# Inner products of text tokens in four 32-column strips instead of one 128-column product

## The chip, the cores and the metric

The kernel runs on one core of one Trainium2 chip. The metric is the device time of one execution in microseconds (us); a kernel's time is the median over its runs. The engines are PE (matrix products; PEld is its weight load), DVE (vector), ACT (scalar), POOL (GpSimd) and SP, which here only issues DMAs.

## The reference

The reference is a cross-attention layer with text tokens and four image-prompt tokens per batch: 8 batches, 112 query rows, 320 channels, 20 heads of 16, 371 text tokens and 4 prompt tokens of 512 numbers each, all float32.

```python
q = heads(hidden_states @ W_q)
k_t = heads(text_ehs @ W_k)
v_t = heads(text_ehs @ W_v)
probs_t = jax.nn.softmax(jnp.einsum('bhsd,bhtd->bhst', q, k_t) * attn_scale, axis=-1)
text_out = jnp.einsum('bhst,bhtd->bhsd', probs_t, v_t)
...
attn_scores = jnp.einsum('bhsd,bhnd->bhsn', q, k_ip) * attn_scale
qsem = _l2norm(jnp.einsum('bhst,bte->bhse', probs_t, text_ehs))
sem = jnp.einsum('bhse,bne->bhsn', qsem, _l2norm(ip_ehs))
probs_ip = jax.nn.softmax(attn_scores + SEM_SCALE * sem, axis=-1)
probs_ip = probs_ip * spatial_mask[None, None, :, None]
out = text_out + jnp.einsum('bhsn,bhnd->bhsd', probs_ip, v_ip)
out = out @ W_out + b_out + residual
```

What matters here is the norm of `qsem`. Its square is p G p, where p is one row of probabilities and G the 371 x 371 matrix of inner products of the batch's text tokens. The kernel computes G once per batch, and uses only its upper triangle, with the entries above the diagonal doubled.

## The kernel before, in words

For each batch the context is transposed into `ctxT`: 128 partitions, 4 chunks `e` of the embedding, 384 token columns, of which 371 are text, 4 are the normalised prompts (L380) and 9 are zero. The 384 tokens are taken in three chunks `c` of 128 rows (NT = 3), and each of these in four blocks `q` of 32 rows (QN = 4, RG = 32), which makes twelve blocks `j` (BLK).

`gram(b)` (L453 to 469, batches 1 to 7) computes the inner products. For each chunk `c` it takes one PSUM bank and issues four products (L461), one per embedding chunk: the weights are the 128 token columns of the chunk, and all columns from the chunk's first to the prompts stream by (375, 247 and 119 of them). They accumulate in the bank. `doubled` (L445) then copies the bank to the tile `ug` on ACT with a factor 2 (L450), and on POOL multiplies the 128 columns of the diagonal chunk with the mask `half` (L451), which has 0.5 in the four diagonal blocks and 1 elsewhere. `half` is set up in the prologue (L172 to 175). Batch 0 has a function of its own, `first_gram`.

`gram_to_groups` (L471) copies 32 rows of `ug` at a time by DMA into `u`, for each of four partition groups: block position `q` of `u` holds those rows for all three chunks. `values` (L525) computes the value vectors into `vext`; `values_to_dram` (L548) writes them to DRAM, all three chunks in one DMA for odd batches, two and then one for even ones; `values_to_groups` (L554) reads them back into `vr`, and `placed` (L602) puts each group's values behind the rows of `u` on POOL (L606). `region(b, c)` (L373) is the part of `u` that belongs to chunk `c`.

A step is one batch and one group of four heads. `product(b, g, j, heads)` (L684, L690) multiplies, for each head `a`, the transposed probabilities of block `j` with `u`'s rows of that block, from the block's diagonal on (L693): 32 partitions of weights per head, so that four heads lie in four row strips of PE's array. `scores` (L639) works in the same strips. The result, 392 columns for block 0 and 40 for block 11, holds p G, the prompts' products, the sum of p and the weighted values.

The order on PE, ACT, POOL, SP and DVE is written out by hand. `pair(n)` (L1125) runs two groups and the scores and probabilities of later ones (two groups ahead); `behind(n)` (L1192) puts what the next batch needs behind every second group: keys (`k`, L499 and L490), queries (`q`, L334), values (`v`, L533), inner products (`gr`), pieces of the finish of the batch before (`f`, L902 and L914). For odd batches the inner products stand between `k` and `v`; for even ones they stand last, behind `f` or `k`, and the next `pair` follows. Behind batch 1's inner products stands the projection of the prompts (L270), whose weights are 32 columns wide. SP's queue carries, in the order written, the probabilities to the transposes (L665), the copies of `ug` (L475), the values (L549, L558), the contexts (L138, L143) and the results (L883).

Of the kernel before, what the change touches and what calls it, by code (L numbers as in the profile page):

```python
# [8 lines left out]
F32 = mybir.dt.float32  # L9
AF = mybir.ActivationFunctionType  # L10
ALU = mybir.AluOpType
# [9 lines left out]
def kernel(  # L21
# [14 lines left out]
    nc = tc.nc  # L36
    P = 128
    B, S, C = x.shape
    T, E = ehs.shape[1:]
# [5 lines left out]
    NE = E // P  # L45
# [5 lines left out]
    RG = 32  # L51
# [11 lines left out]
    QN = P // RG  # L63
# [3 lines left out]
    UCOL = QN * GW  # L67
    assert (H, D, NC, NT, P) == (20, 16, 3, 3, 128) and RG == 2 * D


    groups = [[i * HC + 2 * a + r for a in range(GROUP)] for i in range(2) for r in range(2)]
    groups.append([2 * HC + a for a in range(GROUP)])

    const = ctx.enter_context(tc.tile_pool(name="const", bufs=1))
# [11 lines left out]
    def bank(name, spare=False):  # L86

        tag = turn.pop(0) if turn else "sc" if spare else "mm"
        return pools[tag].tile([P, 512], F32, tag=tag, name=name)
# [79 lines left out]
    make_identity(nc, ident)  # L169
    nc.gpsimd.memset(wq_sb[REST:, FULL, :], 0.0)  # L170

    half = const.tile([P, P], F32, tag="half", name="half")  # L172
    nc.gpsimd.memset(half, 1.0)
    for q in range(QN):
        nc.gpsimd.memset(half[q * RG : (q + 1) * RG, q * RG : (q + 1) * RG], 0.5)

    hmask = const.tile([P, HC], F32, tag="hmask", name="hmask")
    nc.vector.tensor_reduce(
# [28 lines left out]
    k3 = const.tile([P, NT, GROUP, 2, D], F32, tag="k3", name="k3")  # L207

    def more_constants():
        nc.gpsimd.memset(k3[:, :, :, 1, :], 0.0)  # L210
        nc.gpsimd.memset(wo_sb[REST:, FULL, :], 0.0)
        for at in attn_ring:
            nc.gpsimd.memset(at[:, C:], 0.0)
# [137 lines left out]
    st = {}  # L351
# [21 lines left out]
    def region(b, c):  # L373

        u = st[b]["u"].rearrange("p (q w) -> p q w", w=GW)
        return u[:, :, GCOL[c] : GCOL[c + 1]]
# [46 lines left out]
    def first_gram():  # L423

        ctxT = st[0]["ctxT"]
        banks = []
        for c in range(NT):
            banks.append(ps_qd.tile([P, 512], F32, tag="qd", name=f"ps_g_0_{c}"))
            if c == NT - 1:
                nc.gpsimd.tensor_copy(ctxT[:, :, TT:T], ipnT[:, :, :NIP])  # L430
            c0, c1 = c * P, min(c * P + P, T)
            for r in range(c + 1):
                for e in range(NE):
                    nc.tensor.matmul(
                        banks[r][:, c0 - r * P : c1 - r * P],
                        ctxT[:, e, r * P : (r + 1) * P],
                        ctxT[:, e, c0:c1],
                        start=(e == 0),
                        stop=(e == NE - 1),
                    )  # L440
                if c == NT - 1:
                    doubled(banks[r], r)
                yield

    def doubled(ps, c):  # L445

        t0 = c * P
        k = min(P, TT - t0)
        g = ug[:, GCOL[c] : GCOL[c] + T - t0]
        nc.scalar.mul(g, ps[:, : T - t0], 2.0)  # L450
        nc.gpsimd.tensor_tensor(g[:, :k], g[:, :k], half[:, :k], ALU.mult)  # L451

    def gram(b):  # L453

        ctxT = st[b]["ctxT"]

        for c in range(NT):
            t0 = c * P
            ps = bank(f"ps_g_{b}_{c}")
            for e in range(NE):  # L460
                nc.tensor.matmul(  # L461
                    ps[:, : T - t0],
                    ctxT[:, e, t0 : t0 + P],
                    ctxT[:, e, t0:T],
                    start=(e == 0),
                    stop=(e == NE - 1),
                )
            doubled(ps, c)
            yield

    def gram_to_groups(b, blocks):  # L471
# [74 lines left out]
            yield  # L546

    def values_to_dram(b, eng, c0=0, c1=NT):  # L548
        eng.dma_start(  # L549
            st[b]["vd"][c0 * P : c1 * P].rearrange("(c p) x -> p c x", p=P),  # L550
            st[b]["vext"][:, c0:c1, :C],
        )

    def values_to_groups(b):  # L554
        s = st[b]
# [128 lines left out]
    def product(b, g, j, heads):  # L684
        s = st[b]
        xT = s["xT", g]
        banks = s["qd", g]
        c, q = j // QN, j % QN
        for a in heads:
            nc.tensor.matmul(  # L690
                banks[a][:S, j * RG : UW],
                xT[a * RG : (a + 1) * RG, j, :S],
                region(b, c)[a * RG : (a + 1) * RG, q, q * RG :],  # L693
                start=(j == 0),
                stop=(j == BLK - 1),
            )
# [8 lines left out]
    def multiplied(b, g):  # L705

        turned_round = b == B - 1 and g % 2 and g < NG - 1
        products_in(b, g, ("mm", "mm", "sc", "sc") if turned_round else ("qd",) * GROUP)
        for j in range(BLK):
            product(b, g, j, range(GROUP))  # L710
            yield
        del st[b]["xT", g]
# [316 lines left out]
    prompts = normalised_prompts()  # L1029
    context = transposed_context(0)  # L1030
    products = first_gram()
    next(prompts)
    awake(4)
# [10 lines left out]
    run(("q", 0), lambda: project_queries(pairs[0]), 3)  # L1044
    run(("v", 0), None, 2)
    values_to_dram(0, nc.scalar)
    spread(nc.gpsimd, wq_sb)
    nc.gpsimd.tensor_copy(wv_sb[:, :, C:], wk_sb[:, :, FULL * P : C])
# [22 lines left out]
    drain(transposed_context(1))  # L1071
    prompts_behind(1)
    more_constants()
    prologue.close()

# [16 lines left out]
    def gr(b, pieces=1):  # L1092
        run(("g", b), lambda: gram(b), pieces)
# [31 lines left out]
    def pair(n):  # L1125
# [7 lines left out]
        for j in range(BLK - 2):  # L1133
            product(b, g, j, range(GROUP))
            if j < 2:
                heads = (HIGH, LOW)[j]
                coming_scores(n + LEAD, heads, tags[j])
                coming_probabilities(n + LEAD, heads)
            if j == 1:
                transposed(*two, BLK // 2, BLK)  # L1140
            if j % QN == QN - 1:
                placed(*two, (j // QN,))
        products_in(*two, (tags[1],) * 2 + (tags[0],) * 2)
        for there, here in ((HIGH, LOW), (LOW, HIGH)):
            product(*two, 0, there)
            for j in ends:
                product(b, g, j, here)
# [44 lines left out]
    def behind(n):  # L1192
# [31 lines left out]
        elif b % 2 == 0 and g == 2:  # L1224
# [10 lines left out]
            if b == 0:  # L1235
                run(("pp",), None)
            tr(1)
            values_to_dram(nb, nc.sync)
        elif b % 2 == 0:
            new = nb < B - 1  # L1240
# [20 lines left out]
        elif g == 1:  # L1261
            turn[:] = ["qd"] * 4 + ["mm"]
            gram_to_groups(nb, (2,))
            q(b)
            k(b)
            k(nb)
            tr(0)
            f(b - 1)
            v(nb)
            tr(1)  # L1270
            v(nb)
            f(b - 1, 3)
            values_to_dram(nb, nc.sync, 0, 2)
            if b == B - 3:
                prompt_values_by_head()
        else:
            turn[:] = ["qd"] * 3 + ["sc"]
            v(nb)
            f(b - 1)
            values_to_dram(nb, nc.sync, 2)  # L1280
            tr(0)
            k(nb)
            f(b - 1, 2)
            tr(1)
            values_to_groups(nb)
        assert not turn, (b, g, turn)

    for n in range(0, len(steps) - NG, 2):
# [4 lines left out]
        b, g = steps[n]  # L1293
# [16 lines left out]
    b = B - 1  # L1310
# [12 lines left out]
    for g in range(NG):  # L1323
# [20 lines left out]
        if g < NG - 1:  # L1344

            n = GROUP - 1 if g <= LEAD else 1
# [89 lines left out]
```

## Time and profile before

| what | value |
|---|---|
| median of 3 runs | 431.86 us (431.05 to 434.98) |
| the profiled execution | 431.93 us |
| its span, first to last instruction | 430.2 us |
| PE, DVE, ACT, POOL busy | 420.1, 328.3, 190.0, 111.1 us |
| L690, products with u | 216.8 us of PE |
| L461, inner products of batches 1 to 7 | 36.9 us of PE |
| moved by DMA | 64.21 MB |

The span is a little shorter than the time, since the time includes the start and the end of the program. A row of a group names the line, the engine, what it writes and reads, the shape (for PE: rows*columns of the weights, then what streams by), the count, the busy time, the mean of one in ns, and the idle time of the engine before it with what ended it. In the order of time a row starts with its start and its length in us. A row of waits has the sum, the number of times and the longest. PE's instructions overlap, so the length of one is not what it costs; the distance from one start to the next is.

### The profile page before, as it was taken

To read this page: it belongs to the slowest core of one execution; us is meant where nothing else is said; L and a number is where in the kernel's file an instruction comes from. 1 tells how busy PE (TensorE), PEld (TensorE's weight loads), DVE (VectorE), ACT (ScalarE), POOL (GpSimd) and SP (SyncE) were. 2 spreads that over 40 slices of the span, in tenths; PEclk is the share of its full clock that TensorE was granted. 3 is DMA by queue.
4 is the path that set the end of the run, shared out by engine and by line. 5 is a ranking of instruction groups with operands and counts; after the bars stand their busy time and mean duration, and the time that the engine had idled before them with its cause. 6 is when DMAs were issued, how large, how long until landed. Compare 5 with 4: busy or idle time off the path is not lost. (4 is left out here: it accounts for less than half of the span.)

```text
span 430.2 us, 12955 instructions
## 1 busy us (share of the span) xinstructions
PE 420.1 (98%) x5011; PEld 322.3 (75%) x5011; DVE 328.3 (76%) x687; ACT 190.0 (44%) x647; POOL 111.1 (26%) x267
## 2 busy tenths in 40 slices
PE   8999999999999999999999999999999999999986
PEld 8756686878677796868687897768786887776783
DVE  4045387987989886887989897795888897778884
ACT  2254141524632642515543553333643463346793
POOL 4302110021160352021061243002142226026440
PEclk9999999999999999999999999999999999999999
DMA  7669946568564655667644566485754436663300
GB/s 240 182 173 266 216 121 160 159 150 197 137 166 113 175 126 138 170 152 168 173 124 134 163 143 156 141 194 122 171 163 120 127 99 165 180 152 105 95 5 28
DMA packets 57547, 64.21 MB, mean 149 GB/s; under 512 B 18368, under 2 KB 51512, under 8 KB 57486
## 3 DMA queue, kind: packets, MB, share of 16 engines
q1 hardware_dynamic: 56920, 62.66, 57.4%
q8 instruction: 40, 0.66, 0.7%
q10 hardware_dynamic: 566, 0.72, 0.5%
q14 instruction: 21, 0.17, 0.1%
HBM read 18.67 MB, written 5.32 MB: 56 GB/s over the span
## 5 line engine op out<-in xcount | busy, mean ns | idle before, releaser
L690 PE MATMUL ps_qd<-u,xgT 32*112 32x104 f32 (+11 forms) x3840 | 216.8, 352 | 2.0 <-POOL u L606 1.7
L690 PEld LDWEIGHTS ps_qd<-u,xgT 32*112 32x112 f32 x3840 | 182.0, 172 | 35.8 <-issue 8.0
L679 DVE STREAM_TRANSPOSE xgT<-xg 128x768 f32<-128x768 f32 (+1 forms) x63 | 121.2, 1952 | 12.3 <-DMA xg<-p 12.2
L656 ACT ACTIVATE p<-ps_s,nmx 112x371 f32<-112x371 f32 x160 | 85.6, 585 | 54.8 <-DVE nmx L652 53.2
L750 DVE CUSTOM_DVE_ANT_0 junk<-ps_qd,p 112x371 f32<-112x371 f32 x148 | 80.1, 541 | 30.6 <-ACT pvs L717 11.4
L652 DVE TENSOR_REDUCE nmx<-ps_s 112x1 f32<-112x371 f32 x160 | 77.2, 535 | 26.7 <-PE ps_s L639 24.7
L606 POOL COPY u<-vr 128x64 f32<-128x64 f32 x120 | 26.5, 236 | 192.7 <-PE ps_qd L690 111.5
L533 PE MATMUL ps_v<-wv_sb,ctxT 128*128 128x384 f32 (+1 forms) x192 | 63.5, 477 | 0.3 <-ACT kT L506 0.3
L639 PE MATMUL ps_s<-kT,qm 32*112 32x375 f32 (+1 forms) x320 | 62.1, 486 | 1.0 <-ACT shared L735 0.7
L533 PEld LDWEIGHTS ps_v<-wv_sb,ctxT 128*128 128x128 f32 x192 | 35.4, 190 | 20.7 <-ACT kT L506 1.2
L717 ACT COPY pvs<-ps_qd 112x21 f32<-112x21 f32 x150 | 21.3, 199 | 61.3 <-DVE ss L750 60.0
L499 PE MATMUL ps_k<-ctxT,wk_sb 128*128 128x371 f32 x136 | 45.8, 481 | 0.0
L461 PE MATMUL ps_g<-ctxT 128*128 128x375 f32 (+2 forms) x168 | 36.9, 376 | 0.7 <-POOL ctxT L380 0.7
L461 PEld LDWEIGHTS ps_g<-ctxT 128*128 128x128 f32 x168 | 28.2, 191 | 9.7 <-POOL ctxT L380 1.2
L499 PEld LDWEIGHTS ps_k<-ctxT,wk_sb 128*128 128x128 f32 x136 | 24.6, 190 | 13.4 <-issue 0.5
L639 PEld LDWEIGHTS ps_s<-kT,qm 32*112 32x112 f32 x320 | 28.1, 171 | 6.9 <-ACT shared L735 1.3
L540 ACT COPY vext<-ps_v 128x384 f32<-128x384 f32 (+1 forms) x24 | 11.2, 465 | 37.1 <-PE ps_v L533 37.0
L658 ACT COPY ipl<-ps_s 112x4 f32<-112x4 f32 x140 | 24.1, 172 | 0.0
L450 ACT ACTIVATE ug<-ps_g 128x375 f32<-128x375 f32 (+2 forms) x24 | 9.0, 376 | 30.4 <-PE ps_g L461 16.5
L506 ACT COPY kT<-ps_k 128x371 f32<-128x371 f32 x17 | 8.0, 469 | 31.0 <-PE ps_k L499 31.0
L343 DVE TENSOR_SCALAR qm<-ps_q,emask 128x224 f32<-128x224 f32 (+1 forms) x25 | 9.0, 397 | 14.9 <-PE ps_q L334 14.9
L451 POOL TENSOR_TENSOR ug<-ug,half 128x128 f32<-128x128 f32 (+1 forms) x24 | 10.7, 447 | 34.5 <-ACT ug L450 34.3
(161 smaller groups left out, 324.9 us busy)
## 6 DMA issues: line engine op xcount, KB each, us to landing
xg<-p SPq DMA_DIRECT2D x159, 162.3 KB
u<-ug SPq DMA_DIRECT2D x128, 99.0 KB
ct<-in_ctx_dram SPq DMA_DIRECT2D x24, 176.0 KB
vr<-vd SPq DMA_DIRECT2D x32, 120.0 KB
vip<-vipd SPq DMA_DIRECT2D x6, 560.0 KB
vd<-vext SPq DMA_DIRECT2D x4, 480.0 KB
out_dram<-ob SPq DMA_DIRECT2D x8, 140.0 KB
ct<-in_ctx_dram SPq DMA_DIRECT2D x4, 256.0 KB
```

What stands on the lines that cost most here:

```text
L461: nc.tensor.matmul(ps[:, : T - t0], ctxT[:, e, t0 : t0 + P], ctxT[:, e, t0:T], start=(e == 0), stop=(e == NE - 1),)
L499: nc.tensor.matmul(ps[:, :TT], wk_sb[:, e, i * P : (i + 1) * P], s["ctxT"][:, e, :TT], start=(e == 0), stop=(e == NE - 1),)
L533: nc.tensor.matmul(ps[:, :w], ctxT[:, e, c * P : (c + 1) * P], wv_sb[:, e, :w], start=(e == 0), stop=(e == NE - 1),)
L606: nc.gpsimd.tensor_copy(region(b, c)[:, :, UV - c * P :], s["vr"][:, c * QN : (c + 1) * QN, g, :])
L639: nc.tensor.matmul(ps[:S, :w], qm[a * RG : (a + 1) * RG, i, r, j * S : (j + 1) * S], s["kT"][a * RG : (a + 1) * RG, i, :w], start=True, st ...
L652: nc.vector.tensor_reduce(nmx, ps[:S, :TT], AX.X, ALU.max, negate=True)
L656: nc.scalar.activation(p, ps[:S, :TT], AF.Exp, bias=nmx)
L658: nc.scalar.copy(s["ipl"][:, groups[g][a], :], ps[:S, TT:T])
L679: nc.vector.transpose(xT[:, j : j + n].rearrange("p j (k q) -> p q j k", q=QN), xg[:, :, j * RG : (j + n) * RG].rearrange("p q (j k) -> p ...
L690: nc.tensor.matmul(banks[a][:S, j * RG : UW], xT[a * RG : (a + 1) * RG, j, :S], region(b, c)[a * RG : (a + 1) * RG, q, q * RG :], start=(j ...
L717: nc.scalar.copy(s["pvs"][:, h, :], ps[:S, TT:UW])
L750: nc.vector.tensor_tensor_reduce(out=junk, in0=ps[:S, :TT], in1=s["p", g][:, a, :], scale=1.0, scalar=0.0, op0=ALU.mult, op1=ALU.add, accu ...
```

## The change

The product of a chunk's 128 rows becomes four products of 32 rows, each into its own 32 partitions of the same bank. For the first embedding chunk they run over all columns, for the other three only from the block's own diagonal on. The list `DEAL` says which block goes to which 32 partitions: in order for chunks 0 and 2, reversed for chunk 1. What stands below the diagonal is a partial sum that nothing reads. Since the middle chunk's blocks lie in reverse in `ug` and so in `u`, the values are written to DRAM in that order as well (three pieces become six: the reversed chunk goes 32 rows at a time), the mask `half` gets a second version, and `product` looks up the position. Batch 0 keeps its order and its products.

```diff
+    DEAL = ((0, 1, 2, 3), (3, 2, 1, 0), (0, 1, 2, 3))
+
+    def dealt(b, c):
+        return DEAL[c] if b > 0 else DEAL[0]
...
+    half = const.tile([P, 2, P], F32, tag="half", name="half")
+
+    def halves(c):
+        nc.gpsimd.memset(half[:, c, :], 1.0)
+        for p, q in enumerate(DEAL[c]):
+            nc.gpsimd.memset(half[p * RG : (p + 1) * RG, c, q * RG : (q + 1) * RG], 0.5)
+
+    halves(0)
...
     def more_constants():
+        halves(1)
...
             for e in range(NE):
-                nc.tensor.matmul(
-                    ps[:, : T - t0],
-                    ctxT[:, e, t0 : t0 + P],
-                    ctxT[:, e, t0:T],
-                    start=(e == 0),
-                    stop=(e == NE - 1),
-                )
-            doubled(ps, c)
+                for p, q in enumerate(DEAL[c]):
+
+                    s0 = q * RG if e > 0 else 0
+                    nc.tensor.matmul(
+                        ps[p * RG : (p + 1) * RG, s0 : T - t0],
+                        ctxT[:, e, t0 + q * RG : t0 + (q + 1) * RG],
+                        ctxT[:, e, t0 + s0 : T],
+                        start=(e == 0),
+                        stop=(e == NE - 1),
+                    )
+            doubled(ps, c, c % 2)
...
     def values_to_dram(b, eng, c0=0, c1=NT):
...
+        for c in range(c0, c1):
+            q = 0
+            while q < QN:
+                p, n = DEAL[c].index(q), 1
+                while q + n < QN and p + n < QN and DEAL[c][p + n] == q + n:
+                    n += 1
+                to = c * P + p * RG
+                eng.dma_start(
+                    s["vd"][to : to + n * RG], s["vext"][q * RG : (q + n) * RG, c, :C]
+                )
+                q += n
...
         c, q = j // QN, j % QN
+        p = dealt(b, c).index(q)
...
-                region(b, c)[a * RG : (a + 1) * RG, q, q * RG :],
+                region(b, c)[a * RG : (a + 1) * RG, p, q * RG :],
```

More of the change, by code (lines that the diff above doesn't have):

```diff
@@ L170 @@
     nc.gpsimd.memset(wq_sb[REST:, FULL, :], 0.0)
[L172 to L175, printed above, removed]
+    half = const.tile([P, 2, P], F32, tag="half", name="half")
[4 more added lines that the diff above has]
+    halves(0)
     hmask = const.tile([P, HC], F32, tag="hmask", name="hmask")
@@ L441, in first_gram, with doubled @@
                 if c == NT - 1:
-                    doubled(banks[r], r)
+                    doubled(banks[r], r, 0)
                 yield
-    def doubled(ps, c):
+    def doubled(ps, c, h):
         t0 = c * P
@@ L450, in doubled @@
         nc.scalar.mul(g, ps[:, : T - t0], 2.0)
-        nc.gpsimd.tensor_tensor(g[:, :k], g[:, :k], half[:, :k], ALU.mult)
+        nc.gpsimd.tensor_tensor(g[:, :k], g[:, :k], half[:, h, :k], ALU.mult)
     def gram(b):
@@ L548, in values_to_dram @@
     def values_to_dram(b, eng, c0=0, c1=NT):
[L549 to L552, printed above, removed]
+        s = st[b]
+        if b == 0:
+            eng.dma_start(
+                s["vd"][c0 * P : c1 * P].rearrange("(c p) x -> p c x", p=P),
+                s["vext"][:, c0:c1, :C],
+            )
+            return
+        for c in range(c0, c1):
[5 more added lines that the diff above has]
+                to = c * P + p * RG
+                eng.dma_start(
+                    s["vd"][to : to + n * RG], s["vext"][q * RG : (q + n) * RG, c, :C]
+                )
+                q += n
     def values_to_groups(b):
```

## The prediction

> **What bounds the kernel now.** I read the page first (busy time, the 40 slices), then the waits of PE, then the groups by line with shapes kept apart, then the order of time around the changed line.
>
> ```profile
> span 430.2 us, 12955 instructions
> PE 420.1 (98%) x5011; PEld 322.3 (75%) x5011; DVE 328.3 (76%) x687; ACT 190.0 (44%) x647; POOL 111.1 (26%) x267
> PE   8999999999999999999999999999999999999986
> PEclk9999999999999999999999999999999999999999
> PE ps_qd L690 <- POOL u L606: 1.7, 2, 1.0
> PE ps_w L421 <- POOL ident masks.py:199: 1.4, 1, 1.4
> PE ps_g L461 <- POOL ctxT L380: 0.7, 1, 0.7
> ```
>
> PE is busy for 420.1 of 430.2 us, its clock is granted in full in every slice, and its longest waits in sum are 1.7, 1.4 and 0.7 us. So what PE does in a stage decides that stage, and a saving on PE is worth its own size unless something else comes late. The sum is made against the profiled execution: 431.93 us, of which the span is 430.2; the median of the runs shown is 431.86, so the two agree.
>
> The changed work is L461, the inner products of batches 1 to 7.
>
> ```profile
> L461 PE MATMUL ps_g<-ctxT 128*128 128x375 f32 x56 | 19.0, 482 | 0.7 <-POOL ctxT L380 0.7
> L461 PE MATMUL ps_g<-ctxT 128*128 128x247 f32 x56 | 12.8, 372 | 0.0
> L461 PE MATMUL ps_g<-ctxT 128*128 128x119 f32 x56 | 7.3, 274 | 0.0
> L690 PE MATMUL ps_qd<-u,xgT 32*112 32x296 f32 x320 | 30.0, 408 | 0.0
> L690 PE MATMUL ps_qd<-u,xgT 32*112 32x200 f32 x320 | 31.7, 328 | 0.0
> L270 PE MATMUL ps_kv<-wip,ipT 128*32 128x320 f32 x16 | 2.3, 435 | 0.0
> 88.17:93.24 5.07, 5.07 (x25) 1.00 0.94 213
> 41.00:46.27 5.27, 5.27 (x29) 1.00 1.00 264
> 46.27:48.55 2.28, 2.28 (x18) 1.00 1.06 227
> ```
>
> The reader is to see three things. First, 56 per width where the code issues 7 batches x 4 embedding chunks = 28: a float32 product is two passes, each with its own weight load. Second, from 296 to 200 columns a pass gets 80 ns shorter: 0.833 ns per column. Third (the last three rows are stretches of time: length, PE busy), the products of one batch take 5.07 us. Worked out: 2 passes x 4 chunks x (375+247+119) = 5928 columns x 0.833 = 4.94 us, and 0.13 us over 24 passes, some 5 ns each.
>
> **The change, part by part.** *The products themselves.* Each 128-column product becomes four of 32 columns, one per column strip of the array. Whether four strips work side by side, and whether one with less to do runs ahead, decides everything. Side by side is shown for two: L270 has 32-column weights, two products per chunk into partitions 0 and 32. Its 16 passes of 320 columns take 2.28 us in the stretch above; one after the other they need 16 x 0.267 = 4.27 us, two by two 2.13. Running ahead is shown for the four row strips of L690 and L639:
>
> ```profile
> 93.34 1.22 PE L690 MATMUL ps_qd<-u,xgT 32*112 32x392 f32 x10
> 94.10 0.48 PE L639 MATMUL ps_s<-kT,qm 32*112 32x375 f32 x2
> 94.39 0.47 PE L690 MATMUL ps_qd<-u,xgT 32*112 32x360 f32 x2
> 94.41 0.76 PE L639 MATMUL ps_s<-kT,qm 32*112 32x375 f32 x4
> ```
>
> The program (L1133 to 1137) issues four heads' products of block 0, then the scores of heads 2 and 3, then the products of block 1. Block 0 is eight passes; the ten ahead of the first L639 therefore contain two of block 1, which have overtaken scores issued before them. A strip takes its own next piece without regard to the other strips. The Trainium skill says otherwise: in "TensorE: Matmul & The Clock Gate", Part 3, "The mechanism", matmuls start and end strictly in program order. The trace disagrees with it here (ten passes, not eight); the sum by that rule is rival 1's.
>
> With strips independent, a strip's time is the sum of its own widths. Strip 0 has (375+3x375) + (247+3x151) + (119+3x119) = 1500+700+476 = 2676 columns, two passes each. The other strips have 1404+796+380, 1308+892+284 and 1212+988+188. After two chunks of rows all four stand at 2200, against 4 x (375+247) = 2488 today: that is what the mirrored deal does. The last chunk is not balanced, so strip 0 ends last: 5352 column passes x 0.833 = 4.46 us, and 24 passes at 2.5 to 5 ns, 0.06 to 0.13. I take the lower, because the weight load that such passes stand on gets shorter (rows below, 109 for 190 ns): 4.52. Saved: 5.07 - 4.52 = 0.55 us per batch (0.48 with the upper), times 7 = **3.86 us**.
>
> Issuing: 96 passes and 96 loads now stand where 24 and 24 stood. Over 4.52 us that is 47 ns per pass; L690 as a whole runs 3840 passes in 216.8 busy us, 56 ns each, wide and narrow together, and its widths set that pace, not the queue. I take nothing for it; were 56 ns a floor, a batch would take 5.4 us (0.3 more than today, 7 x 0.3 = 2.3 us over the kernel, in place of the saving).
>
> *Changing the shape of the array.* Going from 128-wide to 32-wide weights and back has a price:
>
> ```profile
> L461 PE MATMUL ps_g<-ctxT x168: 265/372/582, 41.0 to 346.5; 128*128 128x375 f32 x56, 128*128 128x247 f32 x56, 128*128 128x119 f32 x56
> L270 PE MATMUL ps_kv<-wip,ipT x16: 432/432/457, 46.3 to 48.2; 128*32 128x320 f32 x16
> L461 PEld LDWEIGHTS ps_g<-ctxT 128*128 128x128 f32 x168 | 28.2, 191 | 9.7 <-POOL ctxT L380 1.2
> L270 PEld LDWEIGHTS ps_kv<-wip,ipT 128*32 128x32 f32 x16 | 0.8, 109 | 1.0 <-issue 0.9
> ...
> 141.94 0.54 PE L490 MATMUL ps_k<-ident,k 128*128 128x128 f32 x3
> 142.32 5.25 PE L461 MATMUL ps_g<-ctxT 128*128 128x375 f32 x24
> 147.40 2.75 PE L533 MATMUL ps_v<-wv_sb,ctxT 128*128 128x384 f32 x8
> ```
>
> The batch at 41.00 (batch 1) comes from row strips, goes on to L270 and takes 5.27 us up to there; the batch at 88.17 comes from L499, full width like itself, and takes 5.07. So an entry with exposed load and an exit cost 0.20 together. By the ranges, the exposed first load costs a full-width pass 582 - 482 = 0.10 us and a 32-wide one 457 - 432 = 0.025; the rest, 0.09 to 0.10, is the array running empty. So: into 32-wide strips 0.12, out of them to full width 0.20, and from full width to row strips the same 0.19 that it costs today. By the order in `behind`: batches 2, 3, 4, 5 and 7 follow full-width work at no cost now, 5 x 0.12 = +0.60. Batch 1 (after L690) and batch 6 (after the 0.7 us wait for L380) pay an exposed load already, and it gets shorter: 2 x -0.08 = -0.16. Batches 3, 5, 7 run into L533 (142.32 to 147.40 shows 5.08 with both ends free): 3 x 0.20 = +0.60. Batches 2, 4, 6 run into row strips, no difference. Batch 1 runs into L270, which has the same shape: -0.12. Sum **+0.92 us**.
>
> *Copies of the values to DRAM.* One or two DMAs per batch become six (the reversed middle chunk goes in four pieces): 7 x 6 - 10 = 32 more on SP's queue.
>
> ```profile
> L549 SPq DMA_DIRECT2D vd<-vext x10: 348/397/483, 73.8 to 369.2; - x10
> L143 SPq DMA_DIRECT2D ct<-in_ctx_dram x24: 225/279/284, 51.0 to 294.2; - x24
> L475 SPq DMA_DIRECT2D u<-ug x128: 507/590/1582, 13.8 to 378.0; - x128
> 312.78 0.40 SPq L549 DMA_DIRECT2D vd<-vext  x1
> 313.23 0.69 SPq L572 DMA_DIRECT2D vipx<-vipd  x1
> 315.06 0.91 SPq L665 DMA_DIRECT2D xg<-p  x1
> ```
>
> A small one costs SP between 0.28 (L143, 19 rows) and 0.59 us (L475, 32 rows); I take 0.40, L549's own row. Four are 1.6 us. Odd batches issue them while the last chunk of vext is still awaited. For the even ones the tightest place is batch 6: behind its copy stands L665, which carries the probabilities to the transposes, and SP stands free from 313.92 to 315.06, 1.1 us. With the first chunk gone early, 1.2 us have to fit there, so L665 is late by 0.1 (0.8 at the upper price). That group is multiplied two groups later, so I count 0; with that cover gone, 0.8 us once. The landing that POOL waits for (vr) hangs on the last chunk's single DMA, which stays.
>
> *Masks.* Five more memsets on POOL at the end of the prologue, ahead of the copies into u.
>
> ```profile
> L175 POOL MEMSET half<- x4: 114/117/119, 2.2 to 2.6; 32x32 f32 x4
> L173 POOL MEMSET half<- x1: 204/204/204, 1.9 to 1.9; 128x128 f32 x1
> POOL u L606 <- PE ps_qd L690: 111.5, 66, 9.1
> ```
>
> That is 0.20 + 4 x 0.12 = 0.67 us, on an engine that waits for PE 111.5 us in all: 0, or 0.7 if a copy of u stood right behind. `doubled` does the same work on ACT and POOL as before; the bank of chunk 1 is done 0.48 us sooner.
>
> Sum: 431.93 - 3.86 + 0.92 = **429.0 us**. The 0.7 us wait at batch 6 stays, since what it waits for is set off by PE's work before it and moves along.
>
> **The rivals.** *1, slower: the four strips do not run at once* (only two share the moving side, or starts keep program order with the two passes of a product together). All strips' widths sum to 10128, x 2 passes x 0.833 and 96 x 2.5 ns = 17.1 us of strip time; two at a time 8.56 per batch, 3.5 more than today: 431.93 + 7 x 3.5 + 0.9 = **457**. A strict order, strip by strip and pass by pass, gives the same 8.56. For it: no row shows four strips with all 128 rows feeding. Against it: L270 with two loses nothing (435 ns a pass at 320 columns, against 436 for full-width L533 of that width), and L690's four overtake. It decides from the point where 17.1 / (5.07 - 0.13) = 3.5 strips are busy on average; below that the kernel is slower.
>
> ```profile
> L533 PE MATMUL ps_v<-wv_sb,ctxT 128*128 128x320 f32 x48 | 13.9, 436 | 0.3 <-ACT kT L506 0.3
> ```
>
> *2, no gain: four at once, but in step*, each round as long as its widest. Then 8 x 0.315 + 8 x 0.208 + 8 x 0.102 = 5.00, saving 0.07 x 7 = 0.5, less than the 0.92: **432.4**. For it: the widths differ by up to 96 columns, and strip 3 has to start chunk 1 seven products ahead of strip 0. Against it: the overtaking above. *3: the saving is there and PE then waits*, for vr or the transposes, at most for the 2.9 us saved: 429 to **432**. Against it: PE's waits on others in mid-kernel are single and under 1.1 us.
>
> **How the numbers follow.** Forecast 0.62, around 429.0 (own range 427.8 to 430.3: the upper pass price gives 429.4, a SP or POOL delay 0.8 more, cheaper shape changes 0.9 less). Rival 1 0.14, of which 0.03 for a partial slowing around 435. Rival 2 0.14. Rival 3 0.10. The range 427.4 to 433.4 holds the forecast and rivals 2 and 3 and leaves out rival 1 and what I have not seen. One per cent is 4.3 us, about what a measurement can tell from no change: faster by more means under 427.5, which even the whole 3.86 with shape changes for nothing (428.1) does not reach, 0.07; slower by more is rival 1 and a little, 0.15; within 0.78.
>
> **What would show it.** The stretch of a batch's products on PE: 4.5 us if right, 5.0 in step, 8.5 if two at a time. L270 starting 0.01 us instead of 0.1 behind batch 1's last pass; L533 starting late by 0.2 behind batches 3, 5 and 7. L461 as 672 passes, in which shapes of different widths stand mixed in time. SP's L665 behind batch 6's copies at most 0.8 us late. The prediction is wrong if four strips feeding from all 128 rows slow each other, if the queue cannot hold a lead of seven products, or if PE's waits grow by what its work shrinks.

## The result, and the profile after

| | kernel before | changed kernel |
|---|---|---|
| median | 431.81 us (430.97 to 435.35, 20 runs) | 434.56 us (431.74 to 437.33, 20 runs) |
| ratio to the kernel before | | 1.0043, 95% interval 1.0025 to 1.0061 |
| profiled execution | 431.93 us, span 430.2 | 432.52 us, span 430.8 |

The change made the kernel slower by 0.4%, where 0.7% faster was forecast. The granted clock is the share of full speed at which PE runs; in some executions it stands at a half for several us (half clock, below), which pulls its mean down. The profiled execution is one of the shorter ones: in 14 of the 20 executions the mean granted clock is under 0.998, and their median is 434.91 us; the other six have 432.69 us.

The lines of the changed code move: L461 is L474 now, L449 to 451 are L459 to 461, L549 is L576, L558 is L585, L606 is L633, L652 and L656 are L679 and L683, L665 is L692, L572 is L599, L475 is L488, L679 is L706, L690 is L718. In the kernels of the experiments they move again, and the names in a row (u, p, xg, vr) tell what it is. First the page of the changed kernel, its busy time and its group of the inner products.

```profile
span 430.8 us, 14013 instructions
PE 418.9 (97%) x5515; PEld 328.2 (76%) x5515; DVE 329.6 (77%) x687; ACT 190.1 (44%) x647; POOL 111.7 (26%) x272
```

PE is busy for 1.2 us less than before, and the span is 0.6 us longer: PE stands idle for 11.9 us, 1.8 more. The shapes of the new passes, kept apart (count, busy time, mean of one in ns, idle time before them):

```profile
L474 PE MATMUL ps_g<-ctxT 128*32 128x375 f32 x98 | 18.9, 485 | 0.0
L474 PE MATMUL ps_g<-ctxT 128*32 128x247 f32 x98 | 13.4, 374 | 0.0
...
L474 PE MATMUL ps_g<-ctxT 128*32 128x55 f32 x42 | 3.4, 216 | 0.0
L474 PE MATMUL ps_g<-ctxT 128*32 128x23 f32 x42 | 2.5, 190 | 0.0
```

A 32-wide pass of 375 columns takes 485 ns, a 128-wide one took 482: four strips that all feed from 128 rows do not slow each other (the order of time and a kernel with full strips, below, show the same from start to start). The order of time on PE around three batches' products (start, length, count):

```profile
42.03 4.61 PE L474 MATMUL ps_g<-ctxT 128*32 128x375 f32 x95
46.42 0.43 PE L280 MATMUL ps_kv<-wip,ipT 128*32 128x320 f32 x1
46.48 0.27 PE L474 MATMUL ps_g<-ctxT 128*32 128x119 f32 x1
46.58 2.32 PE L280 MATMUL ps_kv<-wip,ipT 128*32 128x320 f32 x15
...
90.10 4.71 PE L474 MATMUL ps_g<-ctxT 128*32 128x375 f32 x96
94.74 1.22 PE L718 MATMUL ps_qd<-u,xgT 32*112 32x392 f32 x10
...
144.34 4.71 PE L474 MATMUL ps_g<-ctxT 128*32 128x375 f32 x96
148.98 2.85 PE L546 MATMUL ps_v<-wv_sb,ctxT 128*128 128x384 f32 x8
```

From the first pass to the next work the three batches take 4.39, 4.64 and 4.64 us; before it was 5.27 (41.00 to 46.27), 5.17 (88.17 to 93.34) and 5.08 (142.32 to 147.40). Behind batch 1, where the next work has the same shape, the strips run straight on: a pass of L280 starts at 46.42, ahead of the last pass of L474 at 46.48.

So the saving is there, and it is lost elsewhere. PE's waits show where:

```profile
PE ps_qd L718 <- POOL u L633: 2.6, 3, 1.0
PE ps_qd L718 <- ACT p L683: 1.7, 1, 1.7
```

Before, the first was 1.7 us in two waits, and the wait for p was 0.2 us. The following table goes through PE's order of time: for each stretch, how much longer it is than in the profile of the kernel before (us). The first two columns are the changed kernel in two profiled executions; the other two are kernels from the experiments below.

| stretch | changed | changed again | without the copies | without them, loads moved |
|---|---|---|---|---|
| start to 36 us | +1.03 | +0.96 | +0.32 | +0.76 |
| batch 6's products, with the wait ahead of them | -1.13 | -1.13 | -1.08 | -1.16 |
| the other six batches' products | -2.03 | -2.04 | -1.82 | -2.00 |
| 51 to 63 us | +1.55 | +0.97 | +3.62 | -1.08 |
| 131 to 142 us | +0.41 | 0.00 | 0.00 | 0.00 |
| 330 to 341 us | +0.79 | +0.25 | -0.32 | -0.17 |
| all, to the finish at 417 us | +0.6 | -0.7 | +0.7 | -3.6 |

The first row is chance: a second profile of the unchanged kernel has +1.39 there. The rows add up to the last one within 0.3 us, so the three stretches hold what went wrong. At 51 to 63 us PE waits for p, p waits for DVE's maxima, and these stand behind a transposition that waits for a load. Kernel before, order of time of DVE (in brackets the idle time and what ended it):

```profile
53.91 1.57 DVE L679 STREAM_TRANSPOSE xgT<-xg 128x768 f32<-128x768 f32 x1 [7.06 <-DMA xg<-p]
55.33 1.83 DVE L652 TENSOR_REDUCE nmx<-ps_s 112x1 f32<-112x371 f32 x4
```

Changed kernel:

```profile
55.75 1.56 DVE L706 STREAM_TRANSPOSE xgT<-xg 128x768 f32<-128x768 f32 x1 [7.73 <-DMA xg<-p]
57.17 1.83 DVE L679 TENSOR_REDUCE nmx<-ps_s 112x1 f32<-112x371 f32 x4
```

DVE is idle for 7 us in both: a transfer sets this time, and PE arriving sooner changes nothing. The load came 1.84 us later than in this profile of the kernel before, and not because of the further copies, the first of which stands at 74 us; in a second profile of the kernel before the transposition starts at 55.46 us. At 330 to 341 us the chain is another one. Kernel before, SP and POOL:

```profile
326.26 0.35 SPq L549 DMA_DIRECT2D vd<-vext  x1
329.71 2.92 SPq L558 DMA_DIRECT2D vr<-vd  x4
334.94 0.59 POOL L606 COPY u<-vr 128x64 f32<-128x64 f32 x3 [8.30 <-DMA vr<-vd]
```

Changed kernel, SP, POOL and PE, and behind them a wait of SP's:

```profile
312.47 2.43 SPq L576 DMA_DIRECT2D vd<-vext  x5
314.94 0.69 SPq L599 DMA_DIRECT2D vipx<-vipd  x1
315.73 2.73 SPq L692 DMA_DIRECT2D xg<-p  x3
327.70 0.49 SPq L576 DMA_DIRECT2D vd<-vext  x1
331.30 1.86 SPq L585 DMA_DIRECT2D vr<-vd  x4
335.80 0.59 POOL L633 COPY u<-vr 128x64 f32<-128x64 f32 x3 [9.09 <-DMA vr<-vd]
336.09 3.52 PE L718 MATMUL ps_qd<-u,xgT 32*112 32x392 f32 x56 [0.86 <-POOL u L633]
...
SPq L488 <- DMA vipx<-vipd: 1.6, 1, 1.6
```

Batch 6's first copies hold SP for 2.43 us instead of 0.40, so the load of the prompts' values by head, `vipx`, right behind them is issued 1.71 us later (314.94 against 313.23). A copy of `ug` (L488) then waits 1.6 us for `vipx` to land, which the kernel before does not have to do. The last chunk's copy behind it is issued 1.44 us later (327.70 against 326.26), the loads of vr 1.59 us later, POOL's copies come 0.86 us later, and PE waits 0.86 us, where it had not waited.

### The profile page after: what moved, and what is told of

Read it like the earlier page. It is cut to its first block, busy times and chain, and to the rows that moved or that the text cites. A ratio compares the mean times of both kernels' runs of the same rounds, so it can differ in the third digit from the quotient of the medians.

```text
span 430.8 us, 14013 instructions
## 1 busy us (share of the span) xinstructions
PE 418.9 (97%) x5515; PEld 328.2 (76%) x5515; DVE 329.6 (77%) x687; ACT 190.1 (44%) x647; POOL 111.7 (26%) x272
## 5 line engine op out<-in xcount | busy, mean ns | idle before, releaser
L718 PE MATMUL ps_qd<-u,xgT 32*112 32x104 f32 (+11 forms) x3840 | 217.5, 352 | 4.4 <-POOL u L633 2.6
L718 PEld LDWEIGHTS ps_qd<-u,xgT 32*112 32x112 f32 x3840 | 186.8, 172 | 34.0 <-issue 9.7
L706 DVE STREAM_TRANSPOSE xgT<-xg 128x768 f32<-128x768 f32 (+1 forms) x63 | 122.3, 1969 | 12.8 <-DMA xg<-p 12.8
L683 ACT ACTIVATE p<-ps_s,nmx 112x371 f32<-112x371 f32 x160 | 85.6, 585 | 57.6 <-DVE nmx L679 45.0
L679 DVE TENSOR_REDUCE nmx<-ps_s 112x1 f32<-112x371 f32 x160 | 77.2, 534 | 24.1 <-PE ps_s L666 22.7
L633 POOL COPY u<-vr 128x64 f32<-128x64 f32 x120 | 26.5, 236 | 197.0 <-PE ps_qd L718 113.0
L546 PE MATMUL ps_v<-wv_sb,ctxT 128*128 128x384 f32 (+1 forms) x192 | 63.8, 479 | 0.3 <-ACT kT L519 0.3
L546 PEld LDWEIGHTS ps_v<-wv_sb,ctxT 128*128 128x128 f32 x192 | 35.3, 190 | 21.2 <-ACT kT L519 1.2
L474 PE MATMUL ps_g<-ctxT 128*32 128x119 f32 (+11 forms) x672 | 33.0, 344 | 0.0
L474 PEld LDWEIGHTS ps_g<-ctxT 128*32 128x32 f32 x672 | 26.2, 110 | 6.9 <-issue 3.0
L402 DVE STREAM_TRANSPOSE ctxT<-ct 128x512 f32<-128x512 f32 x18 | 19.2, 1070 | 0.0
```

Of the source, the lines that this page charges most:

```text
L474: nc.tensor.matmul(ps[p * RG : (p + 1) * RG, s0 : T - t0], ctxT[:, e, t0 + q * RG : t0 + (q + 1) * RG], ctxT[:, e, t0 + s0 : T], start=(e ...
L546: nc.tensor.matmul(ps[:, :w], ctxT[:, e, c * P : (c + 1) * P], wv_sb[:, e, :w], start=(e == 0), stop=(e == NE - 1),)
L633: nc.gpsimd.tensor_copy(region(b, c)[:, :, UV - c * P :], s["vr"][:, c * QN : (c + 1) * QN, g, :])
L679: nc.vector.tensor_reduce(nmx, ps[:S, :TT], AX.X, ALU.max, negate=True)
L683: nc.scalar.activation(p, ps[:S, :TT], AF.Exp, bias=nmx)
L706: nc.vector.transpose(xT[:, j : j + n].rearrange("p j (k q) -> p q j k", q=QN), xg[:, :, j * RG : (j + n) * RG].rearrange("p q (j k) -> p ...
```

## The experiments

Three theories were put to the test. A: the 32 further copies hold up SP's queue, and with it what POOL and PE wait for. B: the strips themselves bring the half clock. C: the stretch from 42 to 57 us ends when its transfers have landed, so what PE saves ahead of it is lost there. Each ratio below is to the kernel before, run beside the experiment; its median was 432.10 to 432.89 us in these experiments.

**The six copies alone**, on the kernel before, everything else as it was:

```diff
-        eng.dma_start(vd[c0 * P : c1 * P] ..., vext[:, c0:c1, :C])
+        for c in range(c0, c1):
+            n = 1 if c == 1 else QN
+            for q in range(0, QN, n):
+                eng.dma_start(vd[...: n * RG rows], vext[q * RG : (q + n) * RG, c, :C])
```

> The kernel before with the six copies of the values per batch alone (plain order, middle chunk in four pieces); products, masks and strips as before. Theory A (the 32 extra copies hold up SP's queue, the probabilities and the values read back come late, and PE waits): 2 to 3 us slower than before, PE's waits on POOL for u grow from 1.7 us to 3 or more, granted clock as before. Theory B (the 32-wide strips make the TensorE clock drop in stretches of some executions, which costs about 1.7 us for each 0.004 of mean clock): the same time as before, clock near 1.000. Theory C (the stretch from 42 to 56 us is bound by DMA, and gains ahead of it are lost): no difference from before here.

Measured: 435.33 us, ratio 1.0057 (1.0026 to 1.0089). Its waits of PE, and one of SP:

```profile
PE ps_qd L700 <- POOL u L616: 4.4, 5, 1.3
PE ps_w L421 <- POOL ident masks.py:199: 1.4, 1, 1.4
PE ps_g L461 <- POOL ctxT L380: 1.4, 1, 1.4
...
SPq L475 <- DMA vipx<-vipd: 1.2, 1, 1.2
```

PE waits for POOL's u 2.7 us longer than in the kernel before, and for batch 6's context 0.7 us longer, with not one product changed. SP waits for `vipx` here too, 1.2 us. The copies alone cost 2.5 us by the medians (1.1 to 3.9 by the interval); the mean clock is under 0.998 in 5 of the 12 executions. A stands.

**The change without the copies.** The values go to DRAM as before, and POOL reverses the middle chunk where it places them:

```diff
+            v = s["vr"][:, c * QN : (c + 1) * QN, g, :]
+            if dealt(b, c) != DEAL[0]:
+                v = v[:, ::-1, :]
+            nc.gpsimd.tensor_copy(region(b, c)[:, :, UV - c * P :], v)
```

> The changed kernel with the copies of the values as before (one or two per batch); the middle chunk is put into reverse by POOL where it places the values into u. Theory A: the saving shows, 429 to 430, 0.4 to 0.7% faster than before. Theory B: still slower than before by about 0.5%, with mean clocks of 0.992 in many runs. Theory C: 430 to 431, the saving less that of batch 1 (0.75 us).

Measured: 432.80 us, ratio 1.0004 (0.9972 to 1.0036), beside 434.57 us for the changed kernel again (below). PE's waits for POOL's u are back at 1.7 us. What remains is the stretch at 57 us. PE's longest wait, and three stretches of time (length, busy time of PE, PEld, DVE, ACT and POOL with counts, granted clock, DMA share, GB/s):

```profile
PE ps_qd L705 <- ACT p L670: 2.1, 1, 2.1
```

```profile
55.00:59.90 4.90, 2.81 (x59) 2.35 (x55) 4.47 (x6) 1.95 (x4) 0.24 (x1) 1.00 0.29 63
59.90:63.30 3.40, 3.40 (x32) 3.02 (x30) 2.27 (x9) 0.71 (x4) 0.24 (x1) 0.50 0.69 198
63.30:80.00 16.70, 16.70 (x163) 11.93 (x163) 11.76 (x24) 6.10 (x20) 1.76 (x7) 1.00 0.53 140
```

PE waits for 2.1 us, and from 1.8 us after the wait the clock is granted at a half for 3.4 us, which costs about 1.7 us more: together the +3.62 of the table. So a lost saving can come back as a loss. The mean clock is under 0.998 in 8 of the 12 executions here, in 7 of 12 of the changed kernel and in 8 of 35 of the kernel before beside them.

**Strips with all columns**, straight order, no copies (each strip does the full work, so all four end together):

```diff
-    DEAL = ((0, 1, 2, 3), (3, 2, 1, 0), (0, 1, 2, 3))
+    DEAL = ((0, 1, 2, 3), (0, 1, 2, 3), (0, 1, 2, 3))
...
-                    s0 = q * RG if e > 0 else 0
+                    s0 = 0
```

> As the run with POOL's reversal, but every strip runs over all columns and no block is moved, so PE has the strips and the changes of shape without a shorter sum. Theory A and C: about 1 us slower than before (0.9 for the shapes, some 5.0 us per batch for the products), clock as before. Theory B: 2 to 4 us slower, with clocks of 0.992 in many runs.

Measured: 433.33 us, ratio 1.0001 (0.9975 to 1.0027). A batch's products, order of time on PE, in a stretch at full clock:

```profile
90.71 5.21 PE L474 MATMUL ps_g<-ctxT 128*32 128x375 f32 x96
95.85 1.22 PE L705 MATMUL ps_qd<-u,xgT 32*112 32x392 f32 x10
```

5.14 us from start to start, against 5.17 for 24 full-width passes: 96 passes cost nothing beside 24, and the 0.5 us come from the shortened columns alone. The mean clock is under 0.998 in 2 of the 12 executions, so strips by themselves need not bring half clock.

**The changed kernel again**, beside those three:

> The changed kernel unaltered, for a second profile beside the others on one chip. Theory A: waits of PE on POOL for u at the same two or three places as in the first profile, 433 to 435. Theory B: a stretch of low clock stands in the profile, 434 to 436. Theory C: the long wait of PE at 57 us again, 432 to 434.

Measured: 434.57 us, ratio 1.0025 (0.9987 to 1.0064). Its profile loses 0.97 us at 51 to 63 us.

**Batch 1 in full width**, the kernel without the copies with batch 1's products undivided:

```diff
+                if b == 1:
+                    nc.tensor.matmul(ps[:, : T - t0], ctxT[:, e, t0 : t0 + P], ctxT[:, e, t0:T], ...)
+                    continue
```

> The previous kernel without the extra copies (the reversal of the middle chunk done by POOL), and batch 1's inner products undivided and in full width, batches two to seven in strips. Batch 1's stage lies right ahead of the stretch from 42 to 57 us, in which SP's four loads of xg land late and PE then waits for p. Theory C (that stretch ends when the DMAs have landed, so what batch 1 saves is given back there as a longer wait, and the longer wait lets the granted clock fall): nothing is lost by the undoing; the wait for p at 57 us is about 0.5 us shorter than in the kernel with strips in batch 1, half-clock stretches of 3.4 us come in about a quarter of the executions as with the kernel before, and the time is 430.5 to 431.5 us (0.3 to 0.5% below the kernel before). Theory B (the strips themselves bring the half clock): as often as with seven batches in strips, 432.8 us or more, ratio 1.000 to 1.002.

Measured: 432.36 us, ratio 1.0019 (0.9984 to 1.0054); a mean clock under 0.998 in 6 of 12 executions. The wait for p was 1.2 us, 0.9 less than with strips in batch 1. But neither the median nor the clock came out as C said. The wait differs between executions by more than batch 1's saving of 0.75 us: 1.1, 1.7 and 2.1 us in the three profiles that have this saving, 1.4 us with full columns. So this run does not decide for C.

**The inputs of batches five to seven loaded later**, behind step 4 instead of ahead of the stretch, on the kernel in strips without copies, and as a control on the kernel before:

```diff
-    nc.sync.dma_start(x_sb[:, 5:, :], x[5:].rearrange("b s c -> s b c"))
...
         behind(n)
+        if n == 4:
+            nc.sync.dma_start(x_sb[:, 5:, :], x[5:].rearrange("b s c -> s b c"))
```

> The kernel without the extra copies, all seven batches in strips; the load of the inputs of batches five to seven (420 KB) is moved out of the prologue to behind step 4. Theory C: the loads of xg come about 1.5 us earlier (420 KB by 264 GB/s, the rate at which these slices move data), the wait for p at 57 us shrinks from 2 us to under 0.7 us, the half clock goes with it, and the time is 429.5 to 430.8 us (0.5 to 0.7% below the kernel before). Theory B: the wait shrinks, and the half clock stays as frequent; 431.5 to 432.8 us.

> The control: the kernel before with the same load moved to behind step 4 and nothing else. Its wait for p at 57 us was 0.16 us in the profiled execution. Theory C: little to take away here, 0 to 0.5 us, ratio 0.999 to 1.000. If the move helps the kernel before by 1 us or more, the wait at 57 us is usual there too, and the strips are not what makes it.

Measured: 431.75 us with strips, ratio 0.9975 (0.9947 to 1.0004); 432.26 us for the control, ratio 1.0008 (0.9982 to 1.0034). The wait for p is gone from both profiles (the one with strips has half clock in the finish and took 436.85 us; up to there its clock is full). But PE's stretch from 113 to 131 us grew by 0.99 us and, in the control, by 1.53, with no wait on another engine that accounts for it: the load was only moved to another tight place.

**The kernel before, profiled once more:**

> The kernel before as it is, for a second profiled execution of the stretch from 42 to 57 us. Theory C: the fourth load of xg is issued within 1 us of where it was (45.8 us), and the wait for p stays under 0.7 us. If the wait is 1 us or more here, the 0.16 us of the first profiled execution was chance, and the strips did not lengthen it.

One execution, 433.32 us. Its waits of PE:

```profile
PE ps_qd L690 <- POOL u L606: 1.7, 2, 1.0
...
PE ps_qd L690 <- ACT p L656: 0.3, 1, 0.3
```

The wait for p is 0.3 us where PE comes 1.4 us later than in the first profile, though the fourth load of xg is issued 2.8 us later (48.61 against 45.83 us), more than expected. In the changed kernel it is issued at 49.04 us. So in the kernel before, PE and the transfers come to this place at about the same time, and a kernel that is earlier there by 0.75 us waits.

**The same load in three pieces**, of 140 KB, behind steps 6, 8 and 10; on the kernel in strips without copies, on the kernel before, and, in a third kernel, on strips with PE kept busy at the end (the last line of the edit):

```diff
+        if n in (6, 8, 10):
+            nc.sync.dma_start(x_sb[:, 2 + n // 2, :], x[2 + n // 2])
...
+    awake(3, end=True)
```

> Seven batches in strips, no extra copies, and the inputs of batches five to seven loaded by three transfers of 140 KB behind steps 6, 8 and 10 (first used at about 262 us) instead of one of 420 KB ahead of the stretch from 42 to 57 us. With the single load behind step 4 the wait for p at 57 us was gone, but the stages from 113 to 142 us grew by 1.0 and 0.6 us. Theory C (the strips save 2.9 us, and only what the DMAs hold up behind them eats it): both losses gone, 429.0 to 430.3 us, 0.4 to 0.7% below the kernel before, and the lowest profiled span yet, 427.5 to 428.5 us. Theory B (the strips bring the half clock wherever they stand): no wait at 57 us, and still half or more of the executions with a mean granted clock under 0.998; 430.5 to 432 us.

> The control: the kernel before with the same three transfers. Theory C: its own waits at 57 us were 0.16 and 0.3 us, so 0 to 0.5 us are to be had, 431.4 to 432.2 us, ratio 0.998 to 1.000; the distance to the kernel in strips with the same loads is then the strips' own worth, 1.5 to 2.9 us. If this one falls as far as the kernel in strips does, the loads are the whole gain and the strips are worth nothing.

> The kernel in strips with the three transfers, and three multiplications of the identity by itself (their result is not used) put on PE ahead of the output's transposes at about 416 us, where PE waits 0.8 to 1.8 us for wT. In two profiled executions half clock came right with the longer of these waits (from 418.4 and 424.3 us, 10.2 and 6.8 us of it). If PE's idle time there closes the clock, executions with a mean clock under 0.998 become clearly fewer than without the three (under a quarter of them) and the median falls by 0 to 1.5 us. If the idle time there does not matter, the same share and the same median within 0.3 us.

Measured: 429.06 us with strips, ratio 0.9906 (0.9875 to 0.9936); 433.35 us for the kernel before with the same loads, ratio 0.9999 (0.9970 to 1.0028); 429.37 us with the three multiplications of the identity, ratio 0.9911 (0.9880 to 0.9943). The control's profile is 1.15 us ahead of the kernel before at 417 us, and loses this and more right behind it (columns as above):

```profile
400.00:419.70 19.70, 17.45 (x309) 15.35 (x307) 15.82 (x42) 16.99 (x55) 8.07 (x14) 1.00 0.15 35
419.70:426.60 6.90, 6.90 (x17) 4.53 (x18) 2.78 (x15) 2.72 (x6) 0.00 (x0) 0.51 0.01 2
```

That is half clock for 6.8 us in a kernel without a single strip, and 9 of its 12 executions have a mean clock under 0.998, while of the six with strips none has. B falls. The kernels with and without strips lie 4.3 us apart by the medians, more than the 1.5 to 2.9 expected, because the control loses to half clock. So the profiles are the better measure of the shares: at 417 us the control is 1.15 us ahead of the kernel before (0.8 us from 51 to 63 us, 1.0 at batch 6, 0.2 from 330 to 341, less a start that was 0.8 later), and the kernel with strips 3.6. The loads are a part of the gain, and the strips are worth 2.5 us of it there. The last kernel can't tell whether PE's idle time at the end closes the clock, since the kernel it was built on had no half clock to take away; its own profile has 3.4 us of it, at 28 us.

**The changed kernel with the three loads**, and the kernel without copies once more beside it:

> The changed kernel as it is, copies in reversed order and all, with the inputs of batches five to seven loaded by three transfers behind steps 6, 8 and 10. The 32 further copies cost 2.5 us on the kernel before. Theory A (they hold up SP's queue wherever they stand, and the landings of vr that POOL waits for): they cost 2 to 2.5 us here too, 431.0 to 431.6 us, ratio 0.995 to 0.997, and PE's waits for POOL's u are longer by 1 us or more in all than with POOL doing the reversal (1.7 us). If the copies hurt only together with the late loads of xg at 42 to 57 us, this one comes as low as the kernel without them: 429.1 to 429.8 us.

> The same kernel as the one in strips with three transfers and no further copies, once more, as the measure for the run beside it. Theory C: 428.5 to 429.8 us, ratio 0.988 to 0.993, and few executions with a mean granted clock under 0.998. If theory B holds in part, the lack of half clock in the first six executions was chance, and the median is 430.5 us or more.

Measured: 430.18 us with the copies, ratio 0.9944 (0.9918 to 0.9969); 428.76 us without, ratio 0.9904 (0.9875 to 0.9933). The second repeats the first result. The copies cost 1.4 us by the medians here, though the two intervals overlap; PE's waits for u are 2.0 us with them (first row) and 1.8 without (second), less of a difference than A expected. PE's order of time is 1.0 us longer with them in the three stretches where PE or its weight loads wait for a copy into u (0.4 at 131 to 142 us, 0.3 at 330 to 341, 0.3 at 380 to 400).

```profile
PE ps_qd L718 <- POOL u L633: 2.0, 3, 1.0
```

```profile
PE ps_qd L705 <- POOL u L622: 1.8, 2, 1.0
```

So the two losses are two things, and a part of the copies' cost belongs to the crowded places. The kernel in strips, with POOL doing the reversal and the three loads, is the fastest of the study, 1% faster than the kernel before.

Its span is 426.7 us. The order of time of DVE shows the stretch at 57 us with the load landed 2.9 us earlier than in the changed kernel, and without a wait of PE for p behind it:

```profile
52.83 1.57 DVE L693 STREAM_TRANSPOSE xgT<-xg 128x768 f32<-128x768 f32 x1 [5.07 <-DMA xg<-p]
```

## Why the prediction was wrong, point by point

*The products, -3.86: right.* Behind full-width work a batch's passes take 0.53 us less than before, where 0.55 was forecast. The four strips run at once and each runs ahead on its own, into the next work too. Rivals 1 and 2 are out.

*Changing the shape, +0.92: right but for one term.* Entering 32-wide strips cost 0.09 us (0.12 forecast), running into L546 cost 0.09 at each end of it, 0.18 (0.20 forecast), and batch 1 came to -0.75 in all (-0.55 - 0.08 - 0.12 = -0.75 forecast). The term counted at nothing, "Batches 2, 4, 6 run into row strips, no difference", cost 0.1 to 0.3 us each: the group of products behind them is longer by 0.12, 0.24 and 0.27 us in the changed kernel. With full columns in all strips batch 2's following group was as long as before (0.00), so it is not the shape: the four column strips end at different times, and the row strips that follow are staggered. Behind batch 6 their first passes come 0.20 us earlier to 0.07 us later than in the kernel before, and the group ends with the latest of them.

*"The 0.7 us wait at batch 6 stays, since what it waits for is set off by PE's work before it and moves along": wrong, in the kernel's favour.* It is gone in every profile with strips, and also in the control with three loads. POOL's L380 stands behind three copies into u that wait for a load. Kernel before, SP and POOL:

```profile
279.71 2.15 SPq L558 DMA_DIRECT2D vr<-vd  x4
286.11 0.58 POOL L606 COPY u<-vr 128x64 f32<-128x64 f32 x3 [9.90 <-DMA xg<-p]
286.64 0.19 POOL L380 COPY ctxT<-ipnT 128x16 f32<-128x16 f32 x1
```

The kernel with three loads, second profile:

```profile
276.81 2.15 SPq L571 DMA_DIRECT2D vr<-vd  x4
281.47 0.59 POOL L622 COPY u<-vr 128x64 f32<-128x64 f32 x3 [7.33 <-DMA xg<-p]
283.28 0.20 POOL L390 COPY ctxT<-ipnT 128x16 f32<-128x16 f32 x1 [1.23 <-DVE ctxT L402]
```

Before, the copy of ctxT starts as soon as the copies into u are done; there they are done 1.2 us ahead of it, and it waits for DVE. The wait was set by a transfer, not by PE. In the changed kernel the copies into u start at 285.43 us, earlier than before although the loads of vr are issued 0.88 us later; why they land sooner is not shown. With this wait, the seven batches together saved 3.16 us in the changed kernel, more than the 2.94 forecast; without its 0.7 us, products and shapes saved 2.5, less than forecast, chiefly for the staggering above. That the whole came out so near the forecast is luck.

*The copies, 0: the step that failed.* The prediction put them at "L665 is late by 0.1 (0.8 at the upper price). That group is multiplied two groups later, so I count 0", and "The landing that POOL waits for (vr) hangs on the last chunk's single DMA, which stays". L692 did come only 0.67 us later (315.73 against 315.06), within the upper price, and nobody waited for it. But the prediction priced only L665 (L692). The load between the copies and it, `vipx` (L572, in the prediction's own rows), came 1.71 us later, a copy of `ug` waited 1.6 us for it to land, and with that the last chunk's DMA, which is still a single one, came 1.44 us later, and then the loads of vr, POOL's copies into u and PE. The price of an issue (0.40) was near: five took 2.43 us. What was put at nothing is what the delay does further down the queue, 2.5 us on the kernel before (ratio 1.0057), 1.4 us where the other loads are out of the way.

*Rival 3, 0.10: what happened, and beyond its price.* "PE then waits, for vr or the transposes" was right in both its places, and it was given too little, because PE's waits in the profile were single and short, and this was read as room. The short wait for p at 57 us was the mark of a place where PE and the transfers meet. The saving of batch 1 could not pass it, nor could anything ahead of it. Its price was also too low: it ended at 432, all of the saving lost, while the copies are a loss of their own, and a longer wait can be followed by half clock (+1.7 us).

*"Its clock is granted in full in every slice": true of the one profile, and taken for all executions.* The sum has no term for half clock. With a mean clock under 0.998 in 14 of 20 executions, the changed kernel's median lies 2.0 us above its profile (434.56 against 432.52); this part of the miss has no place in the prediction, in none of its rivals either, and its cause is open.

*Masks, 0: right.* POOL's masks take 0.9 us at 37 us, and its next copy keeps its distance to PE.

What stays open: which executions get half clock. In the profiles it came behind a wait of 2.1 us at 57 us in one, at 28 us in another, and in the finish of three, one of them without strips. That it makes up the 2.2 us between the two medians of the changed kernel's executions fits, but those executions were not profiled. The changed kernel with the three loads has it in 1 of 12, which points to the crowded stretches, but in the control the same loads came with 9 of 12. Why the stretch behind step 4 grows when a load is issued there is open too.

## What to carry to other kernels

A saving on the busiest engine is worth its size only up to the next place where that engine meets a transfer; look for such places by the idle time of the other engines there (DVE's 7 us for a load), not by the small wait of the busy one. An added DMA has to be followed down its queue to the next transfer that somebody waits for, however many instructions further on, and not only to the next one. And moving an early load out of a crowded stretch, in pieces and late enough, can be what makes a saving count: by the medians the strips brought nothing until 420 KB were taken out of their way.

## What the runs showed of the hardware

- Four column strips with weights of 128 rows by 32 columns run side by side at the full rate, and independently: 96 passes of full columns in 5.14 us beside 24 full-width ones in 5.17, and a pass of the next product ahead of the last pass of the one before (46.42 and 46.48 us).
- Row strips that follow column strips of unequal length are staggered, and the group behind them is 0.1 to 0.3 us longer; behind strips of equal length it is as long as before (0.00).
- The clock was halved for 3.4 us, from 1.8 us after a wait of 2.1 us, with PE busy for 2.81 of the 4.9 us before it. A wait of 1.7 us in the changed kernel's profile was followed by none. The Trainium skill, in "TensorE: Matmul & The Clock Gate", Part 1, "What's actually happening", gives a free-running window of 3.4 us, and half rate after at least one idle window. The length agrees with this trace; the condition does not, since the idle time ahead of the half clock was 2.1 us.
- An issue of 32 rows (40 KB) takes SP nearly as long as one of 128 rows: 0.38 to 0.43 us for each of batch 6's four, 0.53 for the one ahead of them, 0.40 for the two chunks in one DMA of the kernel before.
- A later issue on SP's queue can wait for an earlier DMA to land: a copy of `ug` waited 1.6 us for `vipx`, issued 7.9 us and seven other DMAs before it.
